# Five blocks of the third layer's input turned on VectorE in the layer before, and masks loaded in a permuted row order

## Chip, cores and metric

One core of a Trainium2 chip runs one kernel. The metric is device time in microseconds (us) of one launch, the median over several runs.

## What is computed

Four graph layers in a row on N = 4096 nodes with D = 256 features and one adjacency matrix. After each, the input is added and the rows are normalised. The third layer is the one that the change is about:

```python
h = x @ W
e = (h @ a[:D, 0])[:, None] + (h @ a[D:, 0])[None, :]
e = where(e > 0, e, 0.01 * e)
attention = softmax(where(adj > 0, e, -1e12), axis=1)
x = layernorm(x + elu(attention @ h))
```

The first layer has the same form with four heads, the second is multi-head attention with the transposed adjacency as its mask, the fourth attends by cosine similarity of two projections.

## The kernel before

**Tiling.** All of x stays in on-chip memory as X: 32 tiles of 128 nodes, 257 columns. A block is QB = 4 tiles, 512 nodes, so there are NB = 8 blocks and NT = 32 tiles. Each layer loops over chunks b (the 512 nodes whose output is being made) and, inside a chunk, over units j (source tiles). Functions: `additive_heads` (first layer), `multi_head_attention` (second), `additive_one` (third), `Cosine` and `cosine_attention` (fourth).

**Third layer, `additive_one`.** A unit (b, j) is this: `weights` makes 128 sources x 512 targets of unnormalised attention, with an activation on ACT (L456) and a multiplication by the mask on DVE (L458); `sums` runs four accumulating matmuls on PE (L464; fp32 matmuls appear in the trace as two records each). The sums of a unit are issued on PE one unit after its weights. The masks are int32 rows of the transposed adjacency, two source tiles at a time (MJ = 2), so 16 loads of 512 KB per chunk, all on SyncE's queue (SP, L454), into four buffers. A load can start when DVE has finished with the mask four loads earlier.

Before a source tile can be used, its block must be projected: `project` multiplies the transposed block xT by W (L196), and puts h, scaled, into V and the exponentials of the two attention terms into src and dst. `fill_row` then lays src along a row: for blocks 0 and 1 with PE transposes (L446), for the others through DRAM with two DMAs on GpSimd's queue (POOL, L441 and L442). The transposed block comes from `turn`, that is `transposed_block`: eight PE transposes into two PSUM banks (L118) and two copies, on DVE and ACT (L120). Blocks 0 and 1 are turned before the loop; in chunk 0, block n = j // 4 + 2 is turned at j % 4 = 0 and projected at j % 4 = 2.

**A block turned without PE.** `turned_apart` is there already: two VectorE transposes of 32x32 squares (L131), a write of 512 KB to DRAM (`far`, L133) and four reads of 128 KB back (L135), each into 32 partitions. The transposed block that this gives has its nodes in another order: column k*32 + n of tile a is node k*128 + a*32 + n of the block. The second and fourth layers use it.

**The last chunk of the third layer (b = 7)** also prepares the fourth layer for blocks 0 to 5, through `follow.prepare`: step 0 turns X through `turned_apart` on SP's queue into the same pool of three xT buffers, step 1 projects on PE (L869) and normalises rows, step 2 turns the rows through `turned_apart` on POOL's queue into T, with one buffer of squares. It also loads the first masks of the fourth layer on POOL's queue (L854, with a cast), each behind a small copy (`tick`, L91) that holds it back.

**Second layer, `multi_head_attention`.** A unit has scores on PE (L664), an exponential on ACT (L666), the mask on DVE (L676) and sums on PE (L697). Denominators are summed on POOL (L683) for even j and by accumulating DMAs from POOL (L689) for odd j. In one step of the loop come scores and weights of unit i, the sums of unit i - 3, and `finish(b - 1, j)`, a piece of the previous chunk's end, where j is that of the sums; so step j = 44 stands with the weights of unit 47. The rows of block b - 1 get their last scaling at j = 35, 37, 39 and 41. Three PSUM buffers hold scores.

**Order.** In the second layer the order on PE, DVE and ACT is the program's. In the third only PE's is; the other queues are ordered by a planner, which simulates the program. [...]

The functions that the diff touches and their callers, as they were:

Of the kernel before, what the change touches and what calls it, by code (L numbers as in the profile page):

```python
# [9 lines left out]
FP = mybir.dt.float32  # L10
# [8 lines left out]
P = 128  # L19
D = 256  # L20
KC = D // P
QB = 4
QW = QB * P
# [5 lines left out]
def kernel(  # L29
# [27 lines left out]
    nc = tc.nc  # L57
    N = x.shape[0]
    NT = N // P
    NB = N // QW  # L60

    def pool(stack, name, bufs, **kw):
        return stack.enter_context(tc.tile_pool(name=name, bufs=bufs, reuse_waits="tile", **kw))
# [15 lines left out]
    X = feat.tile([P, NT, D + 1], FP, name="X")  # L79
# [40 lines left out]
            copies[c](xT[:, c, :], pt)  # L120
        return xT.rearrange("p c (k i) -> p c k i", i=P)

    def turned_apart(squares, far, part, to, eng):

        B = P // QB
        squares = squares.tile([P, QB, KC, P], FP, name="squares")
        far = far.tile([QB, B, QB, KC * P], FP, name="far")
        for c in range(KC):  # L130
            nc.vector.transpose(squares[:, :, c, :].rearrange("p q (k n) -> p k q n", n=B),  # L131
                                part(c).rearrange("p k (q f) -> p k q f", f=B))
        eng.dma_start(far.rearrange("a f q m -> (a f) (q m)"), squares.rearrange("p q c m -> p (q c m)"))  # L133
        for q in range(QB):
            eng.dma_start(to[q * B:(q + 1) * B], far[:, :, q, :].rearrange("a f m -> f a m"))  # L135
        return to.rearrange("p a (c m) -> p c a m", c=KC)

    def block_apart(sb, once, dr, b, eng):
        xT = sb.tile([P, KC * QW], FP, name="xT").rearrange("p (a m) -> p a m", a=QB)
        return turned_apart(once, dr, lambda c: X[:, b * QB:(b + 1) * QB, c * P:(c + 1) * P], xT, eng)  # L140

    def one_row(mv, k, y):
        st = fin.tile([P, 6], FP, name="bn")
# [29 lines left out]
    def scale_row(y, mv, r, k):  # L173
        nc.vector.tensor_scalar(y, y, mv[:, k, 0:1], r[:, k:k + 1], OP.subtract, OP.mult)
# [226 lines left out]
    def additive_one(w_sb, slope, tail, op, follow):  # L401

        MJ = 2
        mvs, taken = {}, {}
        with ExitStack() as lay:
            keep = pool(lay, "gb_keep", 1)
            V = keep.tile([P, NT, D + 1], FP, name="V")
            src = keep.tile([P, NT, 1], FP, name="src")
# [3 lines left out]
            sb = pool(lay, "gb_sb", 2)  # L412
            xp = pool(lay, "gb_turn", 3)
            sq = pool(lay, "gb_squares", 1)
            far = pool(lay, "gb_far", 2, space=bass.MemoryType.DRAM)
# [3 lines left out]
            dr = pool(lay, "gb_dram", 2, space=bass.MemoryType.DRAM)  # L419

            ps = pool(lay, "gb_ps", 4, space=PSUM)
            pa = pool(lay, "gb_pa", 1, space=PSUM)
            edges = adjT.rearrange("(t p) i -> p t i", p=P)
            mask, acc, prob = {}, {}, {}

# [3 lines left out]
            def turn(b):  # L429
                return transposed_block(xp, bank, b)  # L430

            def project(b, xT, ks=range(QB)):
                groups = [(k, 1, bank().rearrange("p (n f) -> p n f", n=1)) for k in ks]
                additive_values(xT, b, groups, w_sb, V, src, dst, 1, slope)

            def fill_row(b):
                part = row[:, b * QW:(b + 1) * QW]
                if b > 1:

                    far = dr.tile([QB, P], FP, name="far")  # L440
                    nc.gpsimd.dma_start(far.rearrange("k p -> p k"), src[:, b * QB:(b + 1) * QB, 0])  # L441
                    nc.gpsimd.dma_start(part, far.rearrange("k p -> (k p)").unsqueeze(0).to_broadcast([P, QW]))  # L442
                    return
                pr = bank()
                for k in range(QB):
                    nc.tensor.transpose(pr[:, k * P:(k + 1) * P], src[:, b * QB + k, :].to_broadcast([P, P]), ident)  # L446
                nc.scalar.copy(part, pr)

            def weights(b, j):
                cols = slice(b * QW, (b + 1) * QW)  # L450
                m = b, j // MJ
                if j % MJ == 0:
                    mask[m] = mp.tile([P, MJ, QW], I32, name="mask")
                    nc.sync.dma_start(mask[m], edges[:, j:j + MJ, cols])  # L454
                e = sb.tile([P, QW], FP, name="e")
                nc.scalar.activation(e, row[:, cols], AF.Relu, bias=-1.0, scale=dst[:, j, :])  # L456
                prob[b, j] = zp.tile([P, QW], FP, name="prob")
                nc.vector.scalar_tensor_tensor(prob[b, j], e, 1.0, mask[m][:, j % MJ, :], OP.add, OP.mult)  # L458
# [27 lines left out]
            units = [(b, j) for b in range(NB) for j in range(NT)]  # L486
            with tc.manual_schedule(engines={mybir.EngineType.PE}):
                xTs = {0: turn(0), 1: turn(1)}
                project(0, xTs[0])
                project(1, xTs[1], [0, 1])  # L490
                fill_row(0)
                project(1, xTs[1], [2, 3])
                for i in range(len(units) + 1):
                    if i < len(units):
                        b, j = units[i]
                        weights(b, j)

                        if b == 0 and j // QB + 2 < NB:
                            n = j // QB + 2
                            if j % QB == 0:  # L500
                                xTs[n] = turn(n)
                            elif j % QB == 2:
                                project(n, xTs[n])
                                fill_row(n)
                    if i:
                        b, j = units[i - 1]
                        sums(b, j)
                        if (b, j) == (0, 1):
                            fill_row(1)
                        if b == 0 and j in (0, 3, 5):  # L510
                            tail(bank, (0, 3, 5).index(j))
                            if j == 5:
                                follow.start()
                        if b and j % 4 == 0 and j // 4 < QB:
                            outputs(b - 1, j // 4)
                        n, rest = divmod(i - (NB - 1) * NT + 5, 4)
                        if rest == 0 and 0 <= n < NB - 2:
                            follow.prepare(even_bank, n, 0)
                        if b == NB - 1:
                            if j in (6, 10, 14):  # L520
                                follow.load_mask(0, (j - 6) // 4, prob[b, j][:, :1])
# [14 lines left out]
    def multi_head_attention(w_sb, b_sb, tail, rows_of_den, narrow_edges):  # L536
# [8 lines left out]
        MJ = 4  # L545
# [3 lines left out]
        with ExitStack() as lay:  # L549
# [7 lines left out]
            with ExitStack() as pro:  # L557
                wp = pool(pro, "mh_w", 1)
                sb = pool(pro, "mh_in", 4)
                sq = pool(pro, "mh_sq", 1)  # L560
                dr = pool(pro, "mh_far", 2, space=bass.MemoryType.DRAM)
# [79 lines left out]

            zp = pool(lay, "mh_z", 8)
            mp = pool(lay, "mh_mask", 3)
            ps = pool(lay, "mh_pz", 3, space=PSUM)
            pa = pool(lay, "mh_pa", 1, space=PSUM)
            mask, acc, prob, score = {}, {}, {}, {}
# [112 lines left out]
            def finish(b, j):  # L759

                rows = [X[:, b * QB + k, :D] for k in range(QB)]
                if j in (7, 9):
                    join_sums(b, j // 2 - 2)
                elif j == 12:
                    row_sums(halves(), b)
                elif j == 15:
                    bank = halves()
                    pd = turned_row_sums(bank, b)
                    po = turned_half(bank, b, 0)
                    reciprocals(pd, b)  # L770
                    half(po, b, 0)
                elif j == 18:
                    half(turned_half(halves(), b, 2), b, 2)
                elif j in (21, 23, 25, 27):
                    k = (j - 21) // 2
                    if k == 0:
                        mvs[b] = fin.tile([P, QB, 2], FP, name="mv")
                    one_row(mvs[b], k, rows[k])
                elif j == 29:
                    roots[b] = begin_root(mvs[b])  # L780
                elif j == 31:

                    end_root(*roots[b], nc.gpsimd)
                elif j in (35, 37, 39, 41):
                    k = (j - 35) // 2
                    scale_row(rows[k], mvs[b], roots[b][1], k)

# [40 lines left out]
    class Cosine:  # L828

        MJ = 4  # L830
# [192 lines left out]
        return part[:, t:t + QB, :]  # L1023

    w2_sb = const.tile([P, KC, D + 2], FP, name="w2_sb")
    wm_sb, bm_sb = {}, {}
    with ExitStack() as weights1, ExitStack() as den1, ExitStack() as weights3:
        wp = weights1.enter_context(tc.tile_pool(name="w1", bufs=1, side="right"))
# [66 lines left out]
```

## Time and profile before

| What | us |
|---|---|
| median of three runs | 2892.49 (2891.81 to 2894.18) |
| profiled execution, whole | 2892.62 |
| its span on the core | 2890.8 |
| first layer | about 0 to 725 |
| second layer: projections, then the main loop | 725 to 808, 808 to 1708 |
| third layer, its last chunk from 2137 | 1708 to 2213 |
| fourth layer | 2213 to 2891 |

The page gives busy times per engine (PE is TensorE, PEld its weight loads, DVE VectorE, ACT ScalarE, POOL GpSimd, SP SyncE) and the share of the span. The granted clock was 0.999 of full speed. A window row gives the same for a stretch of time. The chain follows the last instruction back through what released it; a row is start, length, what. A group row has the count, the busy time, the mean length of one in ns, and after the second bar the idle time ahead of it with its causes. Times of matmul ends are modelled, so the chain's lengths are better for PE than those of single records.

### The profile page before, as it was taken

The numbers are of one execution on the slowest core, as the hardware profiler recorded it, in microseconds if no ns is written. First come the engines' busy times: TensorE is split into PE (matmuls) and PEld (weight loads), VectorE is DVE, ScalarE is ACT, GpSimd is POOL, SyncE is SP. The second block draws the span as 40 slices with busy tenths as digits, with TensorE's granted clock in tenths as the row PEclk, the third lists the DMA queues.
The fourth block names the chain that finished last, engine by engine and source line by source line (L and its number), as shares of the span: only waits on it lengthen the run. The fifth ranks groups of instructions, "written<-read, shape, count | busy, mean of one in ns | idle before, by whom it ended". The sixth has DMA issues, their size and how long they took to land.

```text
span 2890.8 us, 50566 instructions
## 1 busy us (share of the span) xinstructions
PE 2879.6 (100%) x20093; PEld 1548.7 (54%) x20093; DVE 1959.5 (68%) x2557; ACT 1652.8 (57%) x2582; POOL 945.9 (33%) x705
## 2 busy tenths in 40 slices
PE   9999999999999999999999999999999999999999
PEld 4333333333543333333333358888888777777776
DVE  8899999998777777777777765655667323333333
ACT  7899999997356666666666653444444222222222
POOL 0010010100068988989899870000002000000000
PEclk9999999999999999999999999999999999999999
DMA  7566667675269989889899885565566434333441
GB/s 206 103 139 137 142 134 145 138 133 92 88 138 192 183 187 196 181 187 190 182 193 188 181 178 133 164 184 158 159 185 178 76 57 58 59 58 59 59 59 30
DMA packets 237087, 398.04 MB, mean 138 GB/s; under 512 B 20929, under 2 KB 121265, under 8 KB 235954
## 3 DMA queue, kind: packets, MB, share of 16 engines
q0 software_dynamic: 104320, 184.06, 40.1%
q1 hardware_dynamic: 132112, 210.36, 23.7%
q8 instruction: 157, 2.57, 0.3%
q14 instruction: 80, 0.66, 0.1%
q10 hardware_dynamic: 418, 0.40, 0.0%
HBM read 328.60 MB, written 32.58 MB: 125 GB/s over the span
## 4 chain that ended last, share of the span: by engine, by line
PE 99%; DVE 1%; ACT 0%; DMA 0%; issue 0%; SPq 0%; DVEq 0%
PE acc L293 23%; PE acc L920 15%; PE acc L697 15%; PE p L664 15%; PE acc L464 8%; PE g L464 8%; PE p L912 4%; PE g L912 3%; PE g L579 2%; PE g L196 1%; PE pv L598 1%; PE acc L869 1%; PE acc L196 1%; PE g L118 1%; PE g L305 0%; PE p L734 0%
## 5 line engine op out<-in xcount | busy, mean ns | idle before, releaser
L676 DVE TENSOR_TENSOR prob<-p,mask 128x1024 f32<-128x1024 f32 x512 | 624.0, 1223 | 209.4 <-ACT p L666 203.6
L666 ACT ACTIVATE p<-p,shift 128x1024 f32<-128x1024 f32 x512 | 556.2, 1088 | 325.2 <-PE p L664 324.4
L293 PE MATMUL acc<-prob,V 128*32 128x512 f32 x6144 | 664.0, 593 | 1.1 <-DVE prob L283 1.1
L683 POOL TENSOR_TENSOR den<-den,prob 128x1024 f32<-128x1024 f32 x248 | 626.4, 2526 | 73.9 <-DVE prob L676 66.6
L280 ACT ACTIVATE prob<-row,dst 128x512 f32<-128x512 f32 x1020 | 633.1, 712 | 0.1
L283 DVE SCALAR_TENSOR_TENSOR prob<-prob,mask 128x2048 f32<-128x2048 f32 x256 | 582.7, 2287 | 24.2 <-ACT prob L280 21.3
L664 PE MATMUL p<-qT,kT 64*64 64x512 f32 x4096 | 532.7, 590 | 0.8 <-DVE prob L676 0.8
L697 PE MATMUL acc<-prob,V 64*64 64x512 f32 x4096 | 531.8, 590 | 0.0
L920 PE MATMUL acc<-X,prob 128*128 128x257 f32 x2048 | 485.4, 380 | 0.0
L920 PEld LDWEIGHTS acc<-X,prob 128*128 128x128 f32 x2048 | 389.2, 190 | 161.6 <-issue 112.3
L917 DVE TENSOR_TENSOR prob<-prob,mask 128x512 f32<-128x512 f32 x256 | 176.7, 690 | 405.6 <-ACT prob L916 405.4
L293 PEld LDWEIGHTS acc<-prob,V 128*32 128x32 f32 x6144 | 197.8, 110 | 452.6 <-issue 431.9
L91 POOL COPY tick<-prob 128x1 f32<-128x1 f32 x35 | 40.2, 1150 | 996.0 <-DVE prob L283 644.5
L456 ACT ACTIVATE e<-row,dst 128x512 f32<-128x512 f32 x256 | 184.1, 721 | 241.7 <-DVE prob L458 212.7
L697 PEld LDWEIGHTS acc<-prob,V 64*64 64x64 f32 x4096 | 156.0, 133 | 285.2 <-issue 277.9
L664 PEld LDWEIGHTS p<-qT,kT 64*64 64x64 f32 x4096 | 154.6, 133 | 277.2 <-issue 261.4
L458 DVE SCALAR_TENSOR_TENSOR prob<-e,mask 128x512 f32<-128x512 f32 x256 | 175.5, 686 | 169.8 <-PE acc L464 92.4
L854 POOL DMA_DIRECT2D mask<-in_adjT x64 | 48.1, 751 | 585.2 <-DVE prob L917 523.6
L689 POOL DMA_DIRECT2D den<-prob x240 | 233.2, 972 | 15.7 <-DVE prob L676 6.7
L916 ACT ACTIVATE prob<-p 128x512 f32<-128x512 f32 x144 | 85.7, 596 | 258.4 <-PE p L912 244.3
L464 PE MATMUL acc<-V,prob 128*128 128x257 f32 x1024 | 225.1, 380 | 0.0
L464 PE MATMUL g<-V,prob 128*128 128x257 f32 x1024 | 223.7, 380 | 0.0
(165 smaller groups left out, 1937.1 us busy)
## 6 DMA issues: line engine op xcount, KB each, us to landing
mask<-in_adjT SPq DMA_DIRECT2D x256, 512.0 KB
den<-prob POOLq DMA_DIRECT2D x240, 512.0 KB, 5.1
mask<-edges SPq DMA_DIRECT2D x512, 64.0 KB
mask<-in_adjT POOLq DMA_DIRECT2D x64, 512.0 KB, 5.7
edges<-in_adj POOLq DMA_DIRECT2D x32, 512.0 KB, 9.8
far<-squares SPq DMA_DIRECT2D x16, 512.0 KB
den<-prob SPq DMA_DIRECT2D x16, 512.0 KB
row<-far SPq DMA_DIRECT2D x7, 1024.0 KB
```

What stands on the lines that cost most here:

```text
L280: nc.scalar.activation(z[:, h, :], r, AF.Relu, bias=-1.0, scale=dst[:, j, h:h + 1])
L283: nc.vector.scalar_tensor_tensor(z, z, 1.0, mask[m][:, j % MJ, :].unsqueeze(1).to_broadcast([P, H, QW]), OP.add, OP.mult)
L293: nc.tensor.matmul(acc[b][h * G:(h + 1) * G, n, :], part, prob[b, j][:, h, :], start=(j == 0), stop=(j == NT - 1))
L464: nc.tensor.matmul(acc[b][k][:, :D + 1], prob[b, j][:, k * P:(k + 1) * P], V[:, j, :], start=(j == 0), stop=(j == NT - 1))
L664: nc.tensor.matmul(p[c * d:(c + 1) * d, r, :], kT[half, c, at:at + d], qT[half, c, cols], start=True, stop=True)
L666: nc.scalar.activation(p, p, AF.Exp, bias=shift)
L676: nc.vector.tensor_tensor(z, p, mask[m][:, j % MJ, :].unsqueeze(1).to_broadcast([P, KC, QW]), OP.mult)
L683: nc.gpsimd.tensor_tensor(to, to, flat, OP.add)
L689: nc.gpsimd.dma_start(to, flat, accum_op=OP.add)
L697: nc.tensor.matmul(acc[b][c][r * d:(r + 1) * d, :], V[half, j, r * d:(r + 1) * d], prob[b, j][half, r, :], start=(j == 0), stop=(j == NH - 1))
L912: nc.tensor.matmul(p.rearrange("p (k i) -> p k i", k=QB), T[j // QB][:, 0, j % QB], T[b][:, 1], start=True, stop=True)
L920: nc.tensor.matmul(acc[b][k], prob[b, j][:, k * P:(k + 1) * P], X[:, j, :], start=(j == 0), stop=(j == NT - 1))
```

## The change

In the second layer, chunks 3 to 7 turn blocks 2 to 6 of the new X on VectorE at step 44 and write the squares to DRAM. In the third layer, `fetch` reads these five blocks back on SP's queue in place of the PE turn; block 7 is still turned on PE. fetch(2) comes ahead of the first project; fetch(3) to fetch(6) come at j = 0, 4, 8 and 12 of chunk 0.

Because the fetched blocks have their nodes in the permuted order, the masks of their source tiles are loaded with the same order: four DMAs of 32 partitions each in place of one of 128, for 10 of the 16 masks of a chunk. In the last chunk the quarters with odd k go on POOL's queue, all others on SP's. `fill_row` writes src in four DMAs for the fetched blocks. One buffer for the squares is added to the second layer's memory. The order of the targets (columns of the mask) and of the outputs stays.

```diff
-    def turned_apart(squares, far, part, to, eng):
+    def squares_of(squares, far, part, eng):
...
         eng.dma_start(far.rearrange("a f q m -> (a f) (q m)"), squares.rearrange("p q c m -> p (q c m)"))
+        return far
+
+    def squares_placed(far, to, eng):
+        B = P // QB
         for q in range(QB):
             eng.dma_start(to[q * B:(q + 1) * B], far[:, :, q, :].rearrange("a f m -> f a m"))
         return to.rearrange("p a (c m) -> p c a m", c=KC)
 
+    def turned_apart(squares, far, part, to, eng):
+        return squares_placed(squares_of(squares, far, part, eng), to, eng)
+
+    def chunk(b):
+        return lambda c: X[:, b * QB:(b + 1) * QB, c * P:(c + 1) * P]
+
+    def new_xT(sb):
+        return sb.tile([P, KC * QW], FP, name="xT").rearrange("p (a m) -> p a m", a=QB)
...
+            apart = adjT.rearrange("(b k a n) i -> k n b a i", k=QB, a=QB, n=P // QB)
...
+            def fetch(b):
+                return squares_placed(turned[b], new_xT(xp), nc.sync)
...
-                    far = dr.tile([QB, P], FP, name="far")
-                    nc.gpsimd.dma_start(far.rearrange("k p -> p k"), src[:, b * QB:(b + 1) * QB, 0])
-                    nc.gpsimd.dma_start(part, far.rearrange("k p -> (k p)").unsqueeze(0).to_broadcast([P, QW]))
+                    far = dr.tile([QB, QB, P // QB], FP, name="far")
+                    if b < NB - 1:
+                        for k in range(QB):
+                            at = slice(k * P // QB, (k + 1) * P // QB)
+                            nc.gpsimd.dma_start(far[k].rearrange("a n -> n a"), src[at, b * QB:(b + 1) * QB, 0])
+                    else:
+                        nc.gpsimd.dma_start(far.rearrange("k a n -> (a n) k"), src[:, b * QB:(b + 1) * QB, 0])
+                    nc.gpsimd.dma_start(part, far.rearrange("k a n -> (k a n)").unsqueeze(0).to_broadcast([P, QW]))
...
-                    nc.sync.dma_start(mask[m], edges[:, j:j + MJ, cols])
+                    if j // QB in turned:
+                        for k in range(QB):
+                            eng = nc.gpsimd if b == NB - 1 and k % 2 else nc.sync
+                            eng.dma_start(mask[m][k * P // QB:(k + 1) * P // QB],
+                                          apart[k, :, j // QB, j % QB:j % QB + MJ, cols])
+                    else:
+                        nc.sync.dma_start(mask[m], edges[:, j:j + MJ, cols])
...
                 xTs = {0: turn(0), 1: turn(1)}
+                xTs[2] = fetch(2)
                 project(0, xTs[0])
...
-                            if j % QB == 0:
+                            if j % QB == 0 and n + 1 in turned:
+                                xTs[n + 1] = fetch(n + 1)
+                            elif j % QB == 0 and n + 1 == NB:
                                 xTs[n] = turn(n)
...
+            sq = pool(lay, "mh_squares", 1)
...
+                elif j == 44 and b > 1:
+                    turned[b] = squares_of(sq, turned_far, chunk(b), nc.sync)
...
+    turned = {}
+    turned_far = ctx.enter_context(tc.tile_pool(name="turned", bufs=NB - 3, space=bass.MemoryType.DRAM))
```

More of the change, by code (lines that the diff above doesn't have):

```diff
@@ L136, in turned_apart @@
         return to.rearrange("p a (c m) -> p c a m", c=KC)
+    def turned_apart(squares, far, part, to, eng):
[4 more added lines that the diff above has]
+        return sb.tile([P, KC * QW], FP, name="xT").rearrange("p (a m) -> p a m", a=QB)
     def block_apart(sb, once, dr, b, eng):
-        xT = sb.tile([P, KC * QW], FP, name="xT").rearrange("p (a m) -> p a m", a=QB)
-        return turned_apart(once, dr, lambda c: X[:, b * QB:(b + 1) * QB, c * P:(c + 1) * P], xT, eng)
+        return turned_apart(once, dr, chunk(b), new_xT(sb), eng)
     def one_row(mv, k, y):
```

## The prediction

> **What bounds the kernel now.** I read the page first, then stage windows, then the chain of waits through the third layer's start. Columns of the window rows: stretch, length, then busy us and count for each engine, granted clock, DMA share, GB/s.
>
> ```profile
> PE 2879.6 (100%) x20093; PEld 1548.7 (54%) x20093; DVE 1959.5 (68%) x2557; ACT 1652.8 (57%) x2582; POOL 945.9 (33%) x705
> ```
> ```profile
> 808.00:1708.00 900.00, 899.16 (x8380) 321.49 (x8382) 686.92 (x677) 566.55 (x547) 802.63 (x523) 1.00 0.90 186
> 1719.00:1804.00 85.00, 85.00 (x437) 74.31 (x436) 44.41 (x94) 36.12 (x126) 10.77 (x13) 1.00 0.48 125
> 1804.00:1859.00 55.00, 55.00 (x256) 48.20 (x255) 31.95 (x70) 24.36 (x38) 0.00 (x0) 1.00 0.57 172
> 2137.00:2213.00 76.00, 76.00 (x353) 66.75 (x352) 55.01 (x128) 37.77 (x143) 20.53 (x37) 1.00 0.82 215
> ```
>
> The rows are the second layer's main loop, the third layer's chunk 0, one of its quiet chunks, and its last chunk. PE has no gap worth naming in any of them. So PE work that goes is time that goes, up to the point where its input becomes late; work on the other engines costs nothing until PE waits for it. The chain shows what goes:
>
> ```profile
> 1717.85 1.75 PE g L196 x8
> 1719.59 0.87 PE g L118 x8
> 1720.47 1.74 PE acc L464 x8
> ...
> 1758.63 3.49 PE g L196 x16
> 1762.12 3.47 PE acc L464 x16
> 1765.59 0.87 PE g L118 x8
> 1766.46 3.47 PE acc L464 x16
> ```
>
> Each L118 row is one block turned on PE: 8 transposes, 0.87 us, between matmuls that follow without a gap. Chunk 0 has six such rows (1719.59, 1729.60, 1742.99, 1754.29, 1765.59, 1776.89) for blocks 2 to 7.
>
> [...]
>
> **Part 1, five turns leave PE (L118, blocks 2 to 6).** 5 x 0.87 = 4.35 us at most. Block 7 keeps its turn. The first is not all gain: the timeline has the first weights on DVE at 1719.26 for 0.69, done at 1719.95, and elsewhere PE follows such an end by about 0.2. PE would then stand from 1719.59 to about 1720.15 where it turned until 1720.47: gain 0.3. In the other four, DVE is ahead of PE (DVE's L458 waits for PE L464 in the waits of this stage), so 4 x 0.87 = 3.5. **Sum -3.8 us.** The ten copies to xT (0.68 on DVE, 0.58 on ACT) go too, off the path.
>
> **Part 2, the turns in the second layer.** In each of chunks 3 to 7, at step 44, two L131 transposes run on DVE.
>
> ```profile
> L131 DVE STREAM_TRANSPOSE squares<-X 128x512 f32<-128x512 f32 x28 | 19.5, 701 | 4.9 <-DMA far<-squares 4.6
> ```
>
> That is 1.4 us in DVE's fixed order, behind weights of step 47, ahead of those of step 48. In the timeline, step 47's weights (L676) end at 1230.52 and step 48's start at 1231.07, after 0.55 idle. So step 48's are 0.85 late, ending 1233.15. Who waits: scores of step 51, which reuse that bank, start at 1233.94 on PE. 0.8 is left; the lateness is worked off in two units at about 0.5 idle each. POOL's add for that step is late by the same 0.85; its backlog clears too, though slowly, as an add and a DMA issue (2.53 + 0.97) fill two units of 1.72, and eight prob buffers cover it. The write (512 KB on SP, 0.34 to issue) stands behind DVE in SP's queue, ahead of an L657 mask load; with three mask buffers of four units, that load is due some 9 units (15 us) later. **Taken as 0**; bounds 0 to 5 x 1.4 = 7 if neither cushion held, and no gain is possible.
>
> **Part 3, fetches on SP (20 DMAs, four per block).** An L135 read takes 0.33 to 0.44 of SP when undisturbed. fetch(2) goes ahead of the first mask in SP's queue; that mask is issued at 1710.37 today, once the second layer's last matmul frees the memory, and would go about 1.7 later. First use is at 1719.26, 8.9 after today's issue; the SP rows show no landing, but masks of the same 512 KB read by POOL (L854) land after 5.7 in the median, and 1.7 + 5.7 = 7.4 still fits. The cover is PE's turning and projecting from 1710.28 to 1719.59. xT of block 2 is wanted at 1722.20, about 12 us after the issue. Later fetches are queued six units ahead of their project. **Taken as 0**; if the cover were gone, 1.7 once; a gain is excluded, since no DMA leaves this start.
>
> **Part 4, masks by quarters.** Ten of the 16 masks of each chunk become four DMAs, 320 for 80. The last chunk gives 20 of them to POOL, so SP's 128 mask loads become 48 + 300 = 348. SP's price is 0.37 to 0.46 each, so a quartered mask takes 1.7 of SP per 3.47 us of PE: it fits. A mask is loaded when DVE frees the tile four masks back, which in a quiet chunk is six units, 10.4 us, before use; the whole-mask load is there well within that. That a quarter fills only 32 partitions is no slower by the trace: L135 reads do that, with smaller pieces, four issued within 1.9 us. DVE also waits for four landings in place of one; a satisfied wait takes about 0.04 (the semaphore rows of L135), so three more per mask are nothing against its idle time, 23 of 55 us in a quiet chunk. **Taken as 0** in chunks 0 to 6; upper bound 1 us a chunk. fill_row sends four POOL DMAs for one (5 x 3 = 15 more at 0.76, 11 us of POOL); POOL is busy 10.8 of 85 us there and the rows are first read a chunk later. **0.**
>
> **Part 5, the last chunk, the doubtful place.** POOL's queue here, in the timeline (start, length, instruction, idle before it):
>
> ```profile
> 2160.39 0.75 POOL L91 COPY tick<-prob 128x1 f32<-128x1 f32 x1
> 2160.51 1.32 POOL L854 DMA_DIRECT2D mask<-in_adjT  x1
> 2162.63 0.56 POOL L133 DMA_DIRECT2D far<-squares  x1 [0.80 <-DVE squares L131]
> 2171.16 2.20 POOL L135 DMA_DIRECT2D T<-far  x4 [7.96 <-DMA far<-squares]
> 2173.35 0.57 POOL L133 DMA_DIRECT2D far<-squares  x1
> ```
>
> A quarter behind T (L135) stands up to 8 us until far has landed, then lands itself: a 128 KB read from POOL takes 2.8 to 8.2, median 4.5. Masks are now released 17 to 19 us ahead of use in this chunk (SP issues at 2161.15 what DVE uses at 2178.66). 8 + 2.2 + 1.1 + 4.5 = 15.8: in time, with DVE's own lead over PE behind it, about 2.4 (the weights begun at 2157.88, 0.69 long, feed PE at 2160.97). The other way round, a quarter ahead of far delays it, and DVE's next squares wait until far has landed: the T rows show landing by 2158.2, 2171.2, 2179.6, 2191.5, while the next squares start at 2161.0, 2171.4, 2181.8, 2192.2. Two issues (0.55 each, by the L135 row) may cost DVE 0 to 1 at the two tight places, which that lead hides. **Taken as +0.2**, bounds 0 to 11 (below).
>
> **The sum.** Profiled execution 2892.6 (span 2890.8 and 1.8 around it); -3.8 + 0.2 = 2889.0. The median of the runs, 2892.5, is 0.1 lower, so **2888.9**, -0.12%. About 0.2%, 5.8 us, is what a measurement can tell from no change.
>
> **The rivals.**
> *Slower: POOL's queue becomes the last chunk's limit.* For it: two of four margins above are under 1 us and the DMA share is high. Against it: POOL is busy 20.5 of 76 us. Were both masks of a block (four issues, 2.2) put ahead of each far and its landing 1 us longer, five blocks would add 16; about 2.5 of slack and the lead of 2.4 leave 11: **2900**. It decides from 9.6 lost (5.8 + 3.8), so from 2.9 late per block. Chance 0.18.
> *The second layer slips.* DVE's 1.4 and the extra write meet POOL's adds, the DMA share being 0.90, and each chunk loses 1.4: -3.8 + 7 gives **2895.7**. Against it: the 0.8 left over. Chance 0.05.
> *It does not do what it says:* xT arrives late and PE stands where it turned: **2892.5**. For it, only that the fetch needs SP in order. Chance 0.04.
> *Faster than 5.8 us:* PE has but 4.35 to give; only a better order of the planner could add more. Chance 0.04.
> Forecast: 0.69.
>
> **The numbers.** Range: 2887.0 (all 4.35 and a microsecond of spread) to 2895.5, which takes in the third rival and most of the second. Faster 0.04; same 0.69 + 0.04 + 0.03 = 0.76; slower 0.18 + 0.02 = 0.20.
>
> **What would show it.** L118 in the third layer has one row in chunk 0, and PE stays at its length in every window; at 1719.6 a short gap on DVE's L458. L131 at step 44 without PE idle. In the last chunk, no PE idle and no DVE wait for mask or far DMAs. Wrong, if PE idles after 2137, or the second layer's 900 us grow.

## The result, and the profile after

The change is slower: 2903.5 us median (2902.03 to 2904.15) against 2892.24 (2891.78 to 2894.18) of the kernel before on the same chip, ratio 1.0037, 95% interval 1.0026 to 1.0049. The profiled execution has a span of 2902.2, 11.4 more than before.

The page, PE's entry and the one group that shows where PE now stands (count, then busy us and mean ns, then idle us ahead with its cause):

```profile
PE 2878.9 (99%) x20053; PEld 1543.2 (53%) x20053; DVE 1960.4 (68%) x2562; ACT 1650.2 (57%) x2577; POOL 964.1 (33%) x740
```
```profile
L493 PE MATMUL g<-V,prob 128*128 128x257 f32 x1024 | 226.8, 383 | 11.2 <-DVE prob L487 11.2
```

PE's busy time went down by 0.7 us, not by 4 (slow records, 635 ns in place of 380, count as busy), and it idles 11.2 us ahead of the sums that use the banks of odd chunks (L464 before, L493 now), always for a prob on DVE (L487). The windows tell where: the second layer's main loop, the third layer's chunk 0 and its last chunk.

```profile
808.00:1708.00 900.00, 899.15 (x8380) 321.19 (x8382) 691.74 (x687) 566.54 (x547) 802.69 (x523) 1.00 0.90 189
...
1720.00:1805.00 85.00, 84.14 (x411) 72.70 (x412) 43.49 (x99) 34.09 (x118) 17.41 (x28) 1.00 0.79 168
...
2137.00:2225.00 88.00, 76.81 (x341) 65.91 (x340) 55.74 (x125) 37.06 (x143) 29.89 (x55) 0.94 0.75 194
```

The second layer is full as before. Chunk 0 has lost 0.85. In the last chunk PE stands for 11.2 us and its clock averages 0.94. By the first sums of each chunk in the trace, the change was 2.57 us **ahead** when the last chunk began (2136.72 before, 2134.15 now). It was 11.7 **behind** at the fourth layer's first scores (2212.94, 2224.64). So the last chunk alone lost 14.3: gaps of 1.31, 8.53 and 1.36 (11.2), and about 2.5 at half clock, shown further below; some 0.5 is assigned to nothing.

The chain of waits through the long gap reads backwards from PE:

```profile
2169.51 0.69 DVE prob L487
2170.20 0.63 DVE squares L131
...
2171.12 0.53 POOL far L133
...
2172.55 9.76 DMA mask<-in_adjT
2182.30 2.92 issue
2185.23 0.70 DVE prob L487
...
2185.97 7.75 PE g L493 x24
```

A quarter of a mask leaves POOL at 2172.55, behind far, a tick and a cast. The far was waiting for DVE's squares, and these stood behind the prob of 2169.51, itself late for a quarter from POOL. So the lateness goes round: late mask, late prob, late squares, late far, late next mask. "issue" at 2182.30 hides the other quarter of the same mask, which POOL's timeline shows (start, length, instruction, idle before it):

```profile
2171.12 0.57 POOL L133 DMA_DIRECT2D far<-squares  x1 [1.46 <-DVE squares L131]
2171.68 0.20 POOL L91 COPY tick<-prob 128x1 f32<-128x1 f32 x1
2171.80 0.76 POOL L889 DMA_DIRECT2D mask<-in_adjT  x1
2172.55 0.55 POOL L480 DMA_DIRECT2D mask<-in_adjT  x1
2176.84 2.19 POOL L139 DMA_DIRECT2D T<-far  x4 [3.73 <-DMA far<-squares]
2179.02 1.08 POOL L480 DMA_DIRECT2D mask<-in_adjT  x2
```

The two POOL quarters of one mask (j = 16) are the L480 at 2172.55 and the first at 2179.02; between them stands T, which waits for far to land. The buffer had been free since 2151.39. SP's two quarters went at 2163.40 and 2164.64. The last quarter left 27.6 us after the release and landed at 2185.15, in 6.1; DVE began at 2185.23.

DVE's own order has a share in the gaps, too. Ahead of these weights stand, in one piece, a block's normalisation (rows) and its turn (squares), which wait for PE's step 1:

```profile
2179.08 1.22 DVE L915 TENSOR_TENSOR rows<-rows,r 128x1024 f32<-128x1024 f32 x1
2180.34 1.30 DVE L131 STREAM_TRANSPOSE squares<-rows 128x512 f32<-128x512 f32 x2
2185.23 1.29 DVE L487 SCALAR_TENSOR_TENSOR prob<-e,mask 128x512 f32<-128x512 f32 x2 [3.59 <-issue]
```

In the kernel before, weights stand between these pieces, so PE has sums to do meanwhile:

```profile
2168.27 0.68 DVE L458 SCALAR_TENSOR_TENSOR prob<-e,mask 128x512 f32<-128x512 f32 x1
...
2169.68 1.22 DVE L880 TENSOR_TENSOR rows<-rows,r 128x1024 f32<-128x1024 f32 x1
2170.82 0.69 DVE L458 SCALAR_TENSOR_TENSOR prob<-e,mask 128x512 f32<-128x512 f32 x1
2171.43 1.30 DVE L131 STREAM_TRANSPOSE squares<-rows 128x512 f32<-128x512 f32 x2
```

The late mask is enough for the whole gap of 8.53, since no order can use a mask before it lands. But DVE was free only at 2181.64, so with the same order a mask in time would by these rows still have left a gap of about 4.9 (an estimate). The gap of 1.36 has no wait for a mask ahead of it, only this order. DVE's order is the planner's, and it is not the one of before: the change of the loads moved it.

The half clock shows in windows around that gap: the stand, the 4.4 us after it, and what follows.

```profile
2180.00:2186.00 6.00, 0.03 (x1) 0.03 (x1) 2.38 (x5) 0.05 (x1) 2.30 (x5) 0.53 1.03 267
2186.00:2190.40 4.40, 4.40 (x10) 3.49 (x11) 1.74 (x3) 2.01 (x3) 3.15 (x6) 0.50 0.70 214
2190.40:2200.00 9.60, 9.60 (x45) 8.44 (x44) 3.24 (x8) 4.87 (x21) 1.17 (x3) 0.99 0.54 149
```

PE resumes at a granted clock of 0.50: ten records start within 4.4 us (0.43 apart), afterwards they are 0.217 apart. The 24 records of the chain's last row took 7.75 where 24 x 0.217 is 5.2.

### The profile page after: what moved, and what is told of

The parts are those of the page before. It is cut to its first block, busy times and chain, and to the rows that moved or that the text cites. A ratio compares the mean times of both kernels' runs of the same rounds, so it can differ in the third digit from the quotient of the medians.

```text
span 2902.2 us, 50955 instructions
## 1 busy us (share of the span) xinstructions
PE 2878.9 (99%) x20053; PEld 1543.2 (53%) x20053; DVE 1960.4 (68%) x2562; ACT 1650.2 (57%) x2577; POOL 964.1 (33%) x740
## 3 DMA queue, kind: packets, MB, share of 16 engines
q8 instruction: 157, 2.57, 0.4%
## 4 chain that ended last, share of the span: by engine, by line
PE 97%; DMA 1%; DVE 1%; issue 1%; ACT 0%; POOL 0%; SPq 0%; DVEq 0%; POOLq 0%; ACTq 0%
PE acc L305 23%; PE acc L955 15%; PE acc L730 15%; PE p L697 15%; PE acc L493 7%; PE g L493 7%; PE p L947 4%; PE g L947 3%; PE g L611 2%; PE g L208 1%; PE pv L630 1%; DMA mask<-in_adjT 1%; PE acc L208 1%; PE g L317 0%; PE g L118 0%
## 5 line engine op out<-in xcount | busy, mean ns | idle before, releaser
L716 POOL TENSOR_TENSOR den<-den,prob 128x1024 f32<-128x1024 f32 x248 | 633.5, 2554 | 70.2 <-DVE prob L709 62.9
L295 DVE SCALAR_TENSOR_TENSOR prob<-prob,mask 128x2048 f32<-128x2048 f32 x256 | 582.4, 2286 | 24.2 <-ACT prob L292 21.3
L487 DVE SCALAR_TENSOR_TENSOR prob<-e,mask 128x512 f32<-128x512 f32 x256 | 175.2, 686 | 163.1 <-PE acc L493 74.1
L493 PE MATMUL g<-V,prob 128*128 128x257 f32 x1024 | 226.8, 383 | 11.2 <-DVE prob L487 11.2
L493 PE MATMUL acc<-V,prob 128*128 128x257 f32 x1024 | 224.8, 380 | 1.3 <-DVE prob L487 1.3
```

Of the source, the lines that this page charges most:

```text
L295: nc.vector.scalar_tensor_tensor(z, z, 1.0, mask[m][:, j % MJ, :].unsqueeze(1).to_broadcast([P, H, QW]), OP.add, OP.mult)
L493: nc.tensor.matmul(acc[b][k][:, :D + 1], prob[b, j][:, k * P:(k + 1) * P], V[:, j, :], start=(j == 0), stop=(j == NT - 1))
L716: nc.gpsimd.tensor_tensor(to, to, flat, OP.add)
```

## The experiments

**Theory Q:** the loss is the quarters' place in their queues. In the POOL rows above, T waited 3.73 for far to land, and the two quarters behind it went only at 2179.02, after T. By the theory the same holds for all that stands ahead of quarters (far, T, tick, cast on POOL; far and xT on SP) and waits for something else. **Rivals:** DMA bandwidth or slow landings of POOL's transfers (D); the turns in the second layer; the fetches and xT buffers on SP (X); too few mask buffers. One rival no run excludes: the planner orders DVE, ACT and POOL anew for each version, and no run holds DVE's order fixed.

Each ratio is against the kernel before on the same chip, with its 95% interval; "gaps" is PE's idle time between 1710 and 2260, in pieces of over 0.15 us. The gaps are those of one profiled execution; the runs of v6, v7, v11, v13, v14, v16, v18 and v19 lie 6 to 12 us apart, those of the others within 5, so that in these eight a difference of a few us in the gaps need not be one in the medians. v2, v3 and v4 leave masks in an order that does not belong to the sources: they do the same work, but not the reference's result.

| Run | us | ratio | gaps, all / those that end after 2137 |
|---|---|---|---|
| the change | 2903.5 | 1.0037 [1.0026, 1.0049] | 12.5 / 11.2 |
| v1 second layer's turns only | 2892.28 | 1.0 [0.9991, 1.0009] | 0 / 0 |
| v2 no quarters | 2889.3 | 0.9988 [0.9981, 0.9995] | 0.4 / 0 |
| v3 none in the last chunk | 2891.15 | 0.9993 [0.9984, 1.0002] | 2.3 / 1.0 |
| v4 only in the last chunk | 2900.72 | 1.0027 [1.0017, 1.0038] | 9.0 / 8.3 |
| v5 all on SP | 2909.62 | 1.006 [1.0046, 1.0074] | 15.5 / 14.3 |
| v6 odd on POOL, all chunks | 2917.26 | 1.0087 [1.0073, 1.0101] | 20.7 / 8.3 |
| v7 odd on POOL, not the last | 2916.43 | 1.0078 [1.0064, 1.0091] | 21.9 / 9.3 |
| v11 odd of the last chunk on ACT | 2894.73 | 1.0008 [1.0, 1.0017] | 3.6 / 2.3 |
| v8 six mask buffers | 2922.13 | 1.01 [1.0085, 1.0115] | 24.2 / 22.9 |
| v13 odd on ACT, all chunks | 2893.26 | 1.0005 [0.9996, 1.0013] | 2.8 / 0.6 |
| v14 the same, six buffers | 2896.81 | 1.0014 [1.0007, 1.0021] | 6.8 / 2.8 |
| v15 as v11, six buffers | 2909.72 | 1.0056 [1.0041, 1.0071] | 15.3 / 14.0 |
| v17 T on ACT | 2906.7 | 1.0049 [1.0033, 1.0064] | 13.4 / 12.1 |
| v20 five xT buffers | 2905.55 | 1.0041 [1.0025, 1.0056] | 12.4 / 11.1 |
| v21 masks of four tiles, on SP | 2911.13 | 1.0066 [1.0052, 1.0079] | 16.6 / 12.2 |
| v16 order restored on chip | 2896.83 | 1.0014 [1.0007, 1.002] | 7.0 / 0.2 |
| v18 the same, ACT, five xT | 2894.17 | 1.0003 [0.9995, 1.0011] | 2.9 / 0 |
| v19 the same, five xT | 2893.74 | 1.0005 [0.9997, 1.0013] | 5.2 / 0 |

### Which part: v1, v2, v3, v4

v1 is the kernel before with `turned[b] = squares_of(sq, turned_far, chunk(b), nc.sync)` at j = 44 and nothing in the third layer. The others change one line of the change:

```diff
-                    if j // QB in turned:
+                    if False:                                # v2
+                    if j // QB in turned and b < NB - 1:     # v3
+                    if j // QB in turned and b == NB - 1:    # v4
```

> The kernel before plus the VectorE transposes and the write to DRAM in the second layer, whose result nobody reads. The prediction's part 2 says 0: 2891.5 to 2893, and the second layer's main loop from 809.5 to 1709.7 as before. If DVE's 1.4 us per chunk reach PE: up to 2899.

> The change, but every mask is loaded whole and in the natural row order (one DMA on SP), so masks and permuted source rows do not belong together: the attention weights are those of other edges. This leaves the fetches and takes away all quarters. If removing five PE turns is worth what the sum says, 2888.5 to 2889.5, PE without a gap after 1725. If fetches or the extra waits eat it, 2892.

> Quarters in chunks 0 to 6 as in the change; in the last chunk whole masks in natural row order on SP, which are those of other edges for the fetched blocks. Theory Q (POOL's quarters behind T's reads are the whole loss): 2889 to 2890.5. Theory S (quarters in chunks 0 to 6 fill SP's planned time, so that the fourth layer's turning, step 0, moves into the last chunk and SP stands there for it): still 3 to 10 us of PE idle after 2134, 2893 to 2900.

> Whole masks in natural row order (other edges for the fetched blocks) in chunks 0 to 6; quarters on SP and POOL in the last chunk, as in the change. The turning for the fourth layer then stands in SP's order where it stood before the change. Theory Q: 2899 to 2903, as the changed kernel. Theory S: 2889 to 2891, no PE gap over 1 us in the last chunk. Both needed: in between, with the loss of each alone small.

v1 costs nothing. v2 has the gain, -3.5 by the medians, and no PE gap but the predicted one at the first weights. 
The quarters of chunks 0 to 6 take back 1.9 (v3 over v2): a gap of 0.86 in chunk 0 and one of 1.04 in the last chunk. In chunk 0 it is DVE's order again: in v2 the weights of j = 8, the first from a fetched block, start at 1738.67, ahead of the second layer's last pieces on DVE; in v3 they stand behind these and start at 1742.87, without a wait for a mask. In the last chunk the planner has moved the fourth layer's step 0 (far and xT on SP). Before, and in v2, its far writes went one per chunk, from 1821 and 1817 on; in the change the last four went at 2123, 2133, 2146 and 2163, in v3 at 2122, 2132, 2144 and 2154. v3's chain to the gap of 1.04 runs over POOL: a far that took 11.5 to land, the T behind it and a tick at 2174.26, for which DVE's next weights waited 1.30. That step 0's place makes that far slow is likely, not shown. The quarters of the last chunk alone (v4, where step 0 is early again) cost 11.4 over v2. So most of the loss is made by 20 quarters on POOL and 20 on SP in one chunk. v4's long gap, too, ends with weights that waited 3.65 for their mask.

### Which queue: v5, v6, v7, v11

```diff
-                            eng = nc.gpsimd if b == NB - 1 and k % 2 else nc.sync
+                            eng = nc.sync                                          # v5
+                            eng = nc.gpsimd if k % 2 else nc.sync                  # v6
+                            eng = nc.gpsimd if b < NB - 1 and k % 2 else nc.sync   # v7
+                            eng = nc.scalar if b == NB - 1 and k % 2 else nc.sync  # v11
```

> All quarters on SP in every chunk. POOL is as before the change; the turning of step 0 stands late in SP's order, among 40 quarters. POOL theory alone: as v3, 2890.5 to 2892. If SP standing for DVE's squares and for xT's buffer with four times the loads behind it is as bad as POOL: 2896 to 2903.

> Odd quarters on POOL in all chunks. Step 0's turning comes early, so SP's part of the loss (about 2 us by v3) is gone, and the last chunk has POOL's quarters behind far and T as in v4: 2899 to 2901.5, with PE idle 5 to 9 us in the last chunk. If it is no slower than 2892, POOL's standing is not the cause.

> The whole change, correct order of masks, but the queues the other way round: in chunks 0 to 6 the quarters with odd k go on POOL, in the last chunk all four go on SP. SP's order then has the fourth layer's turning early, as before the change, and POOL has no quarter behind far or T. If POOL's standing in the last chunk is the loss and SP's pushed turning the rest: 2889 to 2890.5, PE without a gap over 1 us. If quarters in the last chunk cost wherever they are issued: 2895 or more.

> As the change, but in the last chunk the odd quarters are issued on ACT's queue, not POOL's. ACT has no far or T to stand for; it has 1 us of idle per unit. If the loss is POOL's standing: like v3, 2890.5 to 2893. If quarters on two queues are late as such, or ACT's own work is held up by waiting for a free mask buffer: 2897 to 2905.

v11 is the cleanest of them: the same DMAs, with only the issuing queue of 20 of them changed, are worth 9.0 us (11.3 over before, then 2.2). SP's far writes of step 0 keep their late places (the last four at 2123, 2133, 2146 and 2162), so these are not what the 9.0 is. DVE's order does change: the weights of j = 14 and 15 now stand ahead of the normalisation, and how much of the 9.0 that gives is open. The median lies above the 2893 that the theory allowed. The trace is that of the fastest run; its last chunk ends at 2212.7, and has the higher DMA share and rate of the two (the change has 0.77 and 204 GB/s in the same stretch):

```profile
2137.00:2213.00 76.00, 73.67 (x340) 64.36 (x339) 54.58 (x126) 35.48 (x141) 20.68 (x37) 1.00 0.85 222
```

More bytes per second and no long gap: bandwidth is not what the change lacked. v5 shows that SP is no refuge: its 2909.6 is worse than either forecast. Its timeline has the standing in the gaps between the starts, ahead of xT, whose far has to land first:

```profile
2149.89 0.37 SPq L133 DMA_DIRECT2D far<-squares  x1
2150.30 2.38 SPq L480 DMA_DIRECT2D mask<-in_adjT  x2
2159.08 1.83 SPq L139 DMA_DIRECT2D xT<-far  x4
```

From 2152.7 to 2159.1 SP issues nothing; the six quarters behind that read go from 2160.95 on. But the weights that end v5's two longest gaps (4.82 and 4.83) do not wait for a mask. They stand behind rows and squares on DVE, as in the change:

```profile
2171.85 1.22 DVE L915 TENSOR_TENSOR rows<-rows,r 128x1024 f32<-128x1024 f32 x1
2173.11 1.31 DVE L131 STREAM_TRANSPOSE squares<-rows 128x512 f32<-128x512 f32 x2
2174.34 1.25 DVE L487 SCALAR_TENSOR_TENSOR prob<-e,mask 128x512 f32<-128x512 f32 x2
```

The last chunk of v7, which has all its quarters on SP as well, has the same gap of 4.82 with the same rows ahead. So with the quarters on SP, the last wait is DVE's planned order; that the planner chose it because it expects SP's quarters late is not shown.

v7 and v6 missed: I had thought POOL free in chunk 0. There, row waits for far<-src to land, and quarters stand behind row:

```profile
1765.93 0.58 POOL L463 DMA_DIRECT2D row<-far  x1 [6.77 <-DMA far<-src]
1766.55 1.07 POOL L480 DMA_DIRECT2D mask<-in_adjT  x2
```

POOL was busy 28 of 85 us there and was still the wrong place for these quarters.

### Is it the lead? v8, v13, v14, v15

```diff
-            mp = pool(lay, "gb_mask", 4)
+            mp = pool(lay, "gb_mask", 6)                                  # v8, v14, v15
-                            eng = nc.gpsimd if b == NB - 1 and k % 2 else nc.sync
+                            eng = nc.scalar if k % 2 else nc.sync                  # v13, v14
+                            eng = nc.scalar if b == NB - 1 and k % 2 else nc.sync  # v15
```

> The change with six mask buffers in the third layer in place of four; nothing else differs. A mask of the last chunk is then released two tiles, some 8 us, earlier. Theory Q (a quarter stands in POOL's in-order queue behind far and T, and the four-buffer lead is too short for two such waits): the 8.5 us gap shrinks to under 2 and the half clock after it goes; what is left is SP's late step 0 (about 1): 2889.5 to 2893. Rival D (the transfers themselves are the limit: POOL's quarters land late because the DMA engines are full): more lead only lets the loads queue longer, the gap stays 4 to 9: 2897 to 2904. Rival O (the planner uses the longer lead to put the quarters behind yet another far): 2898 to 2906.

> The change with the odd quarters on ACT's queue in every chunk, where the change has them on SP in chunks 0 to 6 and on POOL in the last. Theory Q: with neither SP full of quarters nor POOL standing, only the gain of the five turns is left: 2889 to 2891, chunk 0 loses its 0.85 us gap, and the last chunk has gaps under 2 us in all. Rival A (ACT's adds and copies stand behind waits for mask buffers, as POOL's did): chunk 0 loses several us as it did with POOL: 2895 to 2910.

> Odd quarters on ACT's queue in every chunk, and six mask buffers. Theory Q: no PE gap over 0.5 us after 1720: 2888.5 to 2890. Rival A (ACT stands): 2892 to 2905.

> Odd quarters of the last chunk on ACT's queue in place of POOL's, and six mask buffers. Theory Q: the 2.3 us gap that was left with four buffers goes too: 2889 to 2890.5. If what was left came from SP's late step 0 and not from the lead: 2891 to 2894, as with four buffers.

My addition to theory Q, that four buffers give too short a lead, fell: with six, every version is slower, v8 by 18.3 (29.6 over before against 11.3). Rival O was right in kind, its 2906 far too low. POOL's timeline of v8 ahead of its longest gap, 7.59:

```profile
2173.00 2.19 POOL L139 DMA_DIRECT2D T<-far  x4 [4.10 <-DMA far<-squares]
2175.18 0.20 POOL L91 COPY tick<-prob 128x1 f32<-128x1 f32 x1
2175.30 0.77 POOL L889 DMA_DIRECT2D mask<-in_adjT  x1
2176.06 1.61 POOL L480 DMA_DIRECT2D mask<-in_adjT  x3
```

The first two quarters of 2176.06 (j = 14) are for a buffer free since 2144.33. They left 31.7 and more after that and had landed by 2186.81; the weights began at 2186.99, after a wait of 4.33. The freer buffer didn't help these quarters, which stood behind T, a tick and a cast; the order is the planner's, and it came out differently with six. v8 and v15 also begin the last chunk with a gap of 4.17 that no mask makes: step 0's squares stand ahead of the first weights on DVE. So these runs don't try the lead alone. v13 did half of what Q asked: no stand in the last chunk (0.6), but 1.4 in chunk 0, and the median is that of before.

### What stands ahead: v17, v20, v21

v17 has `nc.scalar` for `nc.gpsimd` in the fourth layer's step 2, so far and T leave POOL and the quarters stay. v20 has five xT buffers. v21 has masks of four tiles in three buffers, all on SP, hence half as many quarters of twice the size.

> The change with the fourth layer's step 2 (far and T of blocks 0 to 5) issued on ACT's queue in place of POOL's; the odd quarters stay on POOL, with only ticks and casts beside them. Theory Q (the quarters stood behind far and T): POOL's quarters of the last chunk go out within some 2 us of the release of their buffer, except behind a tick, and the 8.5 us gap goes. But ACT's own activations then stand behind far and T, which may cost as much as it gives: 2891 to 2900. Rival D (POOL's DMAs land too late, whatever stands ahead of them): the quarters are issued early and masks are still late by 4 us or more: 2898 to 2904, with a long landing ahead of the gap in the chain.

> The change with five xT buffers in the third layer in place of three; quarters as in the change. SP no longer stands for an xT buffer ahead of its quarters. Theory Q (POOL's queue makes the 8.5 us gap): it stays at 6 to 9, 2899 to 2904. Rival X (SP's step 0, standing for xT buffers, sets the whole last chunk's pace): gaps fall under 3 us: 2890 to 2896.

> The change with masks of four source tiles (1 MB) in three buffers in place of masks of two in four, and all quarters on SP: a turned block is then four DMAs of 256 KB in place of eight of 128 KB, so 20 in a chunk for 40; natural blocks are loaded by two DMAs of two tiles. POOL has no quarter. Theory Q (what costs is the number of DMAs that have to find a place in a queue that stands for other things): SP's step 0 finds its places again, PE gaps after 2137 under 2 us, 2889.5 to 2893. Rival S (SP stands for far and xT in the last chunk, and what stands behind is late whatever its size): gaps of 4 to 10 there, as with all quarters on SP (13.9 us of gaps, 2909.6): 2896 to 2910.

v17 takes away what stood ahead on POOL, and POOL's quarters go out as soon as their buffers are free: two at 2149.16 (free 2148.87), two at 2157.46 (free 2151.60, behind a tick).

```profile
2149.16 1.07 POOL L480 DMA_DIRECT2D mask<-in_adjT  x2 [0.77 <-DVE prob L487]
2156.21 0.18 POOL L91 COPY tick<-prob 128x1 f32<-128x1 f32 x1 [5.97 <-DVE prob L487]
...
2157.46 1.61 POOL L480 DMA_DIRECT2D mask<-in_adjT  x3
```

The latter two landed by 2163.67, long before the use at 2189.50, and that mask's other two, on SP, had gone by 2168.86. So far and T did hold them, and landing was not the limit. The new gap of 8.15, ahead of the same weights, comes from ACT: its last square (sq) of a block stands behind T, T waits for its far (issued at 2177.23) to land, and DVE's rows and then its weights wait for ACT:

```profile
2186.60 1.77 ACTq L139 DMA_DIRECT2D T<-far  x4
2188.42 0.28 ACT L909 ACTIVATE sq<-acc 128x128 f32<-128x128 f32 x1 [7.08 <-DMA mask<-in_adjT]
...
2188.82 0.69 DVE L910 COPY rows<-acc 128x512 f32<-128x512 f32 x1 [8.29 <-ACT sq L909]
...
2189.50 0.69 DVE L487 SCALAR_TENSOR_TENSOR prob<-e,mask 128x512 f32<-128x512 f32 x1
```

The view puts ACT's wait down to a mask, which ACT does not read; in the order of its queue T stands first. The stand moved to another queue and the time was no better, 2906.7, more than either theory gave. v20 keeps a gap of 7.43 that ends with a late mask, so SP's wait for xT buffers isn't the main cause. v21 says that halving the number of quarters doesn't help on SP: there, too, xT at 2147.75 stands for far, issued at 2137.12. But its two long gaps (4.82 and 4.83) end as v5's do, with weights behind rows and squares on DVE and no wait for a mask. My theory's low figure for it missed, and its 2911.1 is just over the rival's range.

### A version with the gain alone: v16, v18, v19

In v16 a copy on DVE and one on ACT restore the natural order before the projection, so masks are whole and fill_row has two DMAs; the result is the reference's. v19 adds two xT buffers, v18 also puts both copies on ACT.

```diff
+            def natural(raw):
+                xT = new_xT(xp).rearrange("p a m -> p (a m)").rearrange("p (c i) -> p c i", c=KC)
+                for c, copy in enumerate((nc.vector.tensor_copy, nc.scalar.copy)):
+                    copy(xT[:, c, :].rearrange("p (k a n) -> p k a n", k=QB, a=QB),
+                         raw[:, c].rearrange("p a (k n) -> p k a n", k=QB))
+                return xT.rearrange("p c (k i) -> p c k i", i=P)
```

> The five blocks are turned in the second layer and fetched on SP as in the change, but before they are projected, a copy on DVE and one on ACT (each 128x512, as the PE turn had them) put the nodes back in natural order. So all masks are whole loads again, and fill_row has its two DMAs; the result is the reference's. Theory Q (the whole loss comes from the quarters and the queues they stand in): 2888.8 to 2890.3, as with whole masks and no reordering (2889.3); PE gaps after 1720 under 1 us in all. Rival P (the projection waits for fetch and copies in a row, now that a copy stands between): gaps of 0.3 to 1 ahead of each of the five projections: 2890 to 2894. Rival L (the loss comes from the fetches and xT buffers on SP, not from quarters): 2896 or more.

> As v16_reorder_on_chip (whole masks, nodes put in natural order on chip, the reference's result), with two edits: both copies on ACT, because the first DVE copy took 2.57 us beside POOL's addition L743 where the others took 0.42, and five xT buffers in place of three, because raw block and copy hold two of them and the next fetch came late, among the masks. Theory Q (the gain of five turns is there as soon as no quarters are loaded and no input is late): 2888.8 to 2890.5, PE gaps in chunk 0 under 1 us. Rival P (fetches, masks and fill_row's reads meet in chunk 0 whatever the buffers): a gap of 2 to 5 stays there: 2891 to 2897.

> As v16_reorder_on_chip with five xT buffers, copies still one on DVE and one on ACT. If the 4.5 us gap came from the late fetch: it goes and the 1.9 us gap of the slow DVE copy stays: 2890.5 to 2892.5. If buffers don't matter: 2895 to 2898 as with three.

All three have a full last chunk (0 to 0.2 of gaps), without any quarter. All three lose the gain in chunk 0, with a longest gap of 4.49 (v16), 3.34 (v19) or 1.90 (v18); since v18 and v19 have medians within 0.5 of each other, these single traces don't rank them. By its time v16 fell to rival L, and without any quarter a mask is late among the fetches. In v18 the chain has, ahead of the gap:

```profile
1735.50 16.29 DMA mask<-in_adjT
```

One whole mask takes 16 us while fetches, fill_row's reads and other masks are under way; the DMA share of chunk 0 is 0.79, against 0.48 before. v2 has the same fetches and masks, with fill_row's four small DMAs, and no such gap, but it is spared narrowly: the same mask (j = 10) was issued at 1734.71 and used at 1748.12, 13.4 later, after DVE had waited 0.83 for it. Why it was some 3 us quicker stays open. So no version that computes the reference beats the kernel before here; v2's 2889.3 is the best median of all runs.

## Why the prediction was wrong

**Part 1** was right: -3.8 forecast, -3.5 by v2's median (-4.4 by its span). The short stand at the first weights is there, 0.41 up to 1720.0; the chain has one L118 row left in chunk 0, at 1774.32.

**Part 2** was right at 0: PE busy 899.15 of 900, and v1 at 2892.28.

**Part 3** was right at 0 for the change, as v2 shows, though not in the order that it gave: the planner put the first mask (1710.38) ahead of fetch(2) (1710.82). Its cover is thin: with the same fetches v16, v18 and v19 have late masks in chunk 0.

**Part 4** was mis-sized: 0 forecast, 1.9 measured (v3 over v2). "It fits" counted SP's issue time, and "no slower" for 32 partitions rested on issues within 1.9 us, which say nothing of landings. What the quarters changed was the planner's order: the first weights from a fetched block went behind the second layer's last pieces on DVE, and most of step 0 slid into the last chunk.

**Part 5 is the step that failed:** +0.2 forecast; the quarters of the last chunk alone cost 11.4 (v4 over v2), and the last chunk of the change lost 14.3 in the trace, 1.0 of which v3 loses without them. The sum "8 + 2.2 + 1.1 + 4.5 = 15.8: in time" gave a quarter one wait behind far and T. In the trace the last quarter of j = 16 took 33.8 from release to landing: 27.6 in the queue and 6.1 under way. It stood behind the T of three blocks, two fars, two ticks, two casts and the quarters of an earlier mask, and POOL's two quarters of it went to both sides of the last T. The lead was even longer than I took it (25 us up to when PE wanted it). I also held every row of POOL at its time of before, where a late mask delays the squares, and these the next far. DVE's order, too, I held at that of before, where the planner put two weights behind a whole normalisation and turn. And I priced a stand at its length only; the half clock added 2.5.

**The rivals.** "POOL's queue becomes the last chunk's limit" was the right one, at 0.18 too unlikely; its 2900 came from five blocks each 3.2 late, less 4.9 of slack, while the trace has one stand of 8.5, two of 1.3, and a slow clock. What speaks against it in the prediction, POOL busy 20.5 of 76 us, was no argument: in the change POOL is busy 29.9 of 88 us, and a quarter still stood 27.6 in its queue. "The second layer slips" and "does not do what it says" are excluded by v1 and v2.

I had put half of the quarters on POOL to spare SP's issue time (0.37 to 0.46 us each); that the choice of queue changes nothing else but the waits of Part 5 was an assumption of mine, which no trace of before shows. The change did not lack bandwidth: from 2137 to 2213, v11 moved 222 GB/s, the change 204. But between POOL and ACT lay 9.0 us. In the change a quarter stood up to 27.6 us in POOL's queue behind what was ahead of it, and the choice of queue changed the planner's order on DVE.

## What to carry over

Before a DMA is put on a queue, list what stands ahead of it there and what each of these waits for; add these waits, not the issue times, and do it again for every part of a transfer that is split, as the last part decides (DVE began 0.08 us after the last quarter of j = 16 had landed). More buffers (v8) or fewer DMAs (v21) were no cure here. If the waiting rows depend on the work that the DMA feeds, expect the lateness to go round. And where a planner orders the queues, compare the order on the engines that use the data before and after: a load that moves can move their work as well.

## What the runs showed of the hardware

**PE's clock fell after some stands.** After 8.53 us of idle, L493's records last 635 ns in place of 380 for 4.4 us, at a granted clock of 0.50; after 5.12 us (v4) for about 3; after 1.04 (v3) not at all. In between, the length of the stand alone does not decide: after a stand of 2.33 in v20 the clock is 0.50 over the next 2.87 us, and after one of 2.33 in v11 it is 1.00.

```profile
2172.33:2175.20 2.87, 2.87 (x7) 2.32 (x8) 1.14 (x2) 1.42 (x2) 2.08 (x5) 0.50 0.93 232
...
2181.45:2184.45 3.00, 3.00 (x14) 2.66 (x15) 0.54 (x1) 1.31 (x2) 1.01 (x2) 1.00 1.16 249
```

What decides between the two no run here shows. The stand of 8.53 thus cost some 2.5 us more than itself.

**A copy on DVE was long beside an addition on POOL.** In v16 the first 128x512 reordering copy took 2.57 us, the other four about 0.42. The two timelines:

```profile
1721.61 2.57 DVE L451 COPY xT<-xT 128x512 f32<-128x512 f32 x1
...
1728.76 0.42 DVE L451 COPY xT<-xT 128x512 f32<-128x512 f32 x1
```
```profile
1721.34 2.56 POOL L743 TENSOR_TENSOR den<-den 128x1024 f32<-128x1024 f32 x1 [4.96 <-DMA den<-prob]
```

DVE's copy ends 0.28 after POOL's addition. v19 has the same once more: an addition of 2.34 from 1725.70, a copy of 2.23 from 1726.09, which ends 0.28 after it. The other four copies of v16 had no addition on POOL beside them: from 1723.90 to 1800 its timeline holds only the DMAs of fill_row. Why the two go together, no run shows. PE waited 1.9 for v16's long copy, and v18, without it, had only 0.6 there.

**Landings of POOL's loads vary.** In the change's last chunk POOL's quarters and casts together take from 2.5 to 9.8 us, 5.4 in the median. The 20 quarters alone have a median of 4.6, close to the 4.5 that the prediction took from T's reads in the kernel before: the landing was not the term that failed.
